# Layer 1 attention: short blocks of query rows share their buffers of exponentials, fp16 parts and transposed parts

## The chip, the core and the metric

The kernel runs on one core of one Trainium2 chip. The metric is the time of one execution in device microseconds. The numbers in the sections ahead of the result are from the kernel before the change: three timed runs and one profiled execution.

## What is computed

Two layers act on x, of shape (2, 1024, 512) in float32. Each one adds an attention branch and a feed-forward branch to its input, both fed with the layer norm of that input:

```python
xn = _layernorm(x, axis=-1)
x = x + _L0_attn_ref(xn, ...) + _L0_ffn_ref(xn, ...)
xn = _layernorm(x, axis=-1)
x = x + _L1_attn_ref(xn, Wq, Wk_down, Wv_down, Wk_up, Wv_up, Wo) + _L1_ffn_ref(xn, ...)
```

The change is in the attention of layer 1. It has 32 query heads of size 128, and 8 heads of keys and values which are built from a compressed form; four query heads share one head of keys. It is causal:

```python
scores = jnp.einsum('bhqd,bhkd->bhqk', q, k) * scale
scores = jnp.where(causal, scores, -1000000000.0)
attn = jax.nn.softmax(scores, axis=-1)
out = jnp.einsum('bhqk,bhkd->bhqd', attn, v)
return out.transpose(0, 2, 1, 3).reshape(b, s, H * D) @ Wo.T
```

## The kernel before

**Arithmetic.** float32 values are held as two fp16 parts, a high and a low one, and each product takes three matmul passes (`mm3`, recorded at L88): high by high, high by low, low by high.

**Units of work in layer 1.** The outer loop runs over 16 groups: 2 batches of 8 key heads. A group has 32 steps (`s`), and each step takes one *row block*: 32 query positions of the four heads, which makes 128 rows. Row block `s` sees `32 * (s + 1)` keys, so W goes from 32 to 1024 within a group. Four row blocks make one column `c` (`c = s // 4`, 0 to 7) of 128 query positions.

**One row block**, in the order in which it passes the engines:

- TensorE: scores into a PSUM bank `s` (four banks; L88 with `s<-K,Q`).
- VectorE: scale, mask and running minimum into the float32 buffer `P` (L268; above 512 keys also L272), with the minimum in `nm`.
- ScalarE: exponential in place, with the row sum (L276).
- VectorE: reciprocal (L289). ScalarE: times a constant (L290), then the high part into `Phl` (L295).
- GpSimd: a memset of the part of `Phl` that lies past W, up to the next multiple of 128 (L285; three of four row blocks need one).
- VectorE: the low part into `Phl` (L301), which reads `P` and `Phl`.
- SyncE's queue: a DMA that transposes `Phl` into `PT` (L303).
- TensorE: probabilities times values, per pair of row blocks (`group_av`, L328, into the one PSUM bank `av`). ScalarE and VectorE write that out as two parts `ao` (`evac`, L103 and L104), and TensorE multiplies `ao` by Wo (`wo_block`, L88 with `pp<-wo,ao`); VectorE adds the result to `acc` (L707).

**Buffers.** `T(tag, shape, bufs=n)` takes one of n buffers of that tag, and each is as large as the largest tile of the tag. `P` has 3, `Phl` has 3, `PT` has 3. One row block takes a whole `P` and a whole `Phl`, whatever its W. A pair of row blocks takes one `PT`. A buffer is free again when every instruction that used it is done: `P` after the low part (L301), `Phl` after the transposing DMA has landed, `PT` after `group_av`. So row block `s` needs the `P` and the `Phl` of row block `s - 3`, and pair j needs the `PT` of pair j - 3.

**Order.** The program names the work step by step: row block `s` in step `s`; the low part of the block before it in the same step; `group_av` of a pair three or four steps later (`AVD = 5`); `wo_block` three steps after that (`WOD = 10`). The projections of queries (`qproj`), of the next group's keys and values (`kv`) and the loads and splits of weights on GpSimd (`load_w`, `split_pool`, L94 to L96, L662) are hung on steps too. In the eight groups of batch 0 there is more of it: the Sinkhorn chain of layer 0's second batch on GpSimd and VectorE (`sk`, L522 to L564), its mixing on ScalarE and GpSimd (L613, L614), gating, the low-rank feed-forward block (`ffn_block`, L907, L912). When the program is built, a scheduler orders the instructions of each engine by a timeline of its own, in which a step waits where a buffer isn't free. On the chip each engine then runs its instructions in that fixed order and waits for semaphores.

## Time and profile before

| | |
|---|---|
| three timed runs | 1926.15, 1918.57, 1919.13 us; median 1919.13 |
| profiled execution | 1926.57 us, its span 1924.8 us |
| TensorE busy | 1743.7 us, 91% of the span, 11458 matmuls |
| VectorE busy | 1487.2 us, 77% |
| ScalarE busy | 1204.1 us, 63% |
| GpSimd busy | 902.4 us, 47% |
| first scores of layer 1 | at 268 us; the groups of batch 1 begin at 1147 us |

Read it so. All times in the traces count from the start of the span. A line of waits gives the engine that waited, its instruction, what ended the wait, the microseconds in total, how often, and the longest. A line of the timeline gives the start, the length, the engine, the line, the operation with its tiles, and in square brackets how long the engine was idle before it and what ended that. A line of a table of stretches gives the length and, for each engine, busy time with the number of instructions, then the granted TensorE clock (1.00 is full), the DMA engines' busy share and GB/s. Ends of matmuls are modelled.

### The profile page before, as it was taken

What the parts mean: (1) busy time and instruction counts of PE and PEld (TensorE: products, weight loads), DVE (VectorE), ACT (ScalarE), POOL (GpSimd) and SP (SyncE); (2) the same over time, 40 slices, a digit from 0 to 9 for tenths busy, and PEclk for the clock granted to TensorE, in tenths of its full rate; (3) what the DMA queues carried; (4) which work ended last, traced back from release to release, by engine and by line L of the source; (5) the groups of instructions that cost most, each with busy time, mean ns of one, the idle gap of its engine ahead of it and who ended that gap; (6) DMA issues with size and microseconds to landing.
All of it is one profiled execution on the core that took longest, in us unless ns stands there. A gap on an engine that the chain in (4) does not pass through costs nothing. (4 is left out here: it accounts for less than half of the span.)

```text
span 1924.8 us, 35319 instructions
## 1 busy us (share of the span) xinstructions
PE 1743.7 (91%) x11458; PEld 1050.0 (55%) x11458; DVE 1487.2 (77%) x4050; ACT 1204.1 (63%) x2917; POOL 902.4 (47%) x1540
## 2 busy tenths in 40 slices
PE   4766399999999989999899899999999999999998
PEld 3433146556556555555554456666566666656565
DVE  8888967987887868686965767777778787878675
ACT  4747755656566777866444556666666666666564
POOL 5657676676756554634612715151515152426100
PEclk9877799999999999999989999999999999999999
DMA  7425225566553746475744855665656565557455
GB/s 203 88 45 132 56 65 110 137 126 124 108 128 87 157 92 139 109 137 123 151 96 77 173 110 126 132 116 132 126 125 129 127 135 118 131 121 147 106 120 118
DMA packets 707308, 230.27 MB, mean 120 GB/s; under 512 B 689953, under 2 KB 690081, under 8 KB 707122
## 3 DMA queue, kind: packets, MB, share of 16 engines
q1 hardware_dynamic: 691666, 180.75, 46.3%
q0 software_dynamic: 13152, 43.07, 8.7%
q10 hardware_dynamic: 2304, 4.20, 0.7%
q8 instruction: 90, 1.47, 0.3%
q14 instruction: 96, 0.79, 0.2%
HBM read 52.81 MB, written 4.19 MB: 30 GB/s over the span
## 5 line engine op out<-in xcount | busy, mean ns | idle before, releaser
L301 DVE SCALAR_TENSOR_TENSOR Phl<-P,r,Phl 128x1024 f16<-128x1024 f32 (+31 forms) x515 | 469.8, 917 | 180.1 <-ACT Phl L295 168.4
L276 ACT ACTIVATE P<-P,nm 128x1024 f32<-128x1024 f32 (+31 forms) x528 | 392.3, 743 | 319.1 <-DVE nm L268 302.2
L328 PE MATMUL av<-PT,V 128*128 128x256 f16 x3648 | 456.6, 277 | 21.5 <-DMA PT<-Phl 13.0
L88 PE MATMUL s<-K,Q 128*128 128x512 f16 (+22 forms) x2400 | 446.8, 317 | 31.0 <-DVE P L272 19.5
L295 ACT ACTIVATE Phl<-P,r 128x1024 f16<-128x1024 f32 (+31 forms) x515 | 374.1, 733 | 109.1 <-DMA PT<-Phl 92.1
L328 PEld LDWEIGHTS <-V 128*128 128x128 f16 x3648 | 359.4, 99 | 121.8 <-DMA PT<-Phl 16.1
L88 PE MATMUL pp<-wo,ao 128*128 128x512 f16 x1536 | 373.6, 380 | 20.3 <-ACT ao L103 20.1
L285 POOL MEMSET Phl<- 128x192 f16 (+2 forms) x384 | 77.6, 205 | 657.1 <-DMA PT<-Phl 515.9
L88 PE MATMUL pp<-xT,wq 128*128 128x512 f16 x1536 | 375.1, 383 | 0.0
L88 PEld LDWEIGHTS <-Q 128*128 128x128 f16 x2400 | 222.9, 98 | 185.5 <-issue 44.6
L88 PEld LDWEIGHTS <-ao 128*128 128x128 f16 x1536 | 148.0, 98 | 175.9 <-ACT ao L103 27.7
L88 PEld LDWEIGHTS <-wq 128*128 128x128 f16 x1536 | 150.5, 99 | 169.1 <-issue 8.2
L268 DVE CUSTOM_DVE_ANT_0 P<-s,mask,nm 128x272 f32<-128x272 f32 (+15 forms) x256 | 157.0, 615 | 7.3 <-DVE P L272 1.0
L272 DVE TENSOR_SCALAR_CACHE_REDUCE P<-s 128x512 f32<-128x512 f32 (+15 forms) x272 | 152.0, 561 | 7.6 <-PE s L88 4.2
L94 POOL TENSOR_SCALAR f2k<-f2k 128x512 f32<-128x512 f32 x164 | 115.3, 704 | 88.0 <-DMA f2k<-in_Wq 46.3
L289 DVE RECIPROCAL r<-r 128x1 f32<-128x1 f32 x528 | 80.5, 156 | 77.2 <-ACT P L276 71.5
L290 ACT ACTIVATE r<-r 128x1 f32<-128x1 f32 x528 | 95.8, 193 | 66.6 <-DVE r L289 65.1
L268 DVE CUSTOM_DVE_ANT_0 P<-s,mask 128x32 f32<-128x32 f32 (+15 forms) x256 | 106.3, 430 | 13.2 <-PE s L88 10.6
L88 PEld LDWEIGHTS <-xT 128*128 128x128 f16 x864 | 65.1, 104 | 80.1 <-DMA xT<-h2k 43.5
L88 PE MATMUL pp<-cmp,xT 128*128 128x128 f16 (+2 forms) x720 | 88.1, 277 | 20.5 <-DMA xT<-h2k 15.8
L104 DVE SCALAR_TENSOR_TENSOR Q<-pp,Q 128x512 f16<-128x512 f32 x128 | 87.1, 681 | 25.3 <-ACT Q L103 25.2
L103 ACT ACTIVATE ao<-av 128x512 f16<-128x512 f32 x128 | 74.7, 584 | 47.6 <-PE av L328 47.3
(262 smaller groups left out, 2137.6 us busy)
## 6 DMA issues: line engine op xcount, KB each, us to landing
f2k<-in_Wq POOLq DMA_DIRECT2D x64, 256.0 KB, 3.4
f2k<-in_WoT POOLq DMA_DIRECT2D x64, 256.0 KB, 3.6
PT<-Phl SPq DMA_TRANSPOSE x528, 3.4
acc<-in_x SPq DMA_DIRECT2D x16, 256.0 KB, 5.2
f2k<-in_Wup POOLq DMA_DIRECT2D x16, 256.0 KB, 3.5
out<-acc ACTq DMA_DIRECT2D x16, 256.0 KB, 3.1
xr<-in_x SPq DMA_DIRECT2D x12, 256.0 KB, 5.1
f2k<-in_Wlat POOLq DMA_DIRECT2D x8, 256.0 KB, 6.5
```

The lines of the kernel that those rows point to most:

```text
L88: nc.tensor.matmul(dst, lhs(l), rhs(r), start=(i == 0 and j == 0), stop=(i == n - 1 and j == 2))
L94: G.tensor_scalar(stage, stage, scale, 1.0, ALU.mult, ALU.mult)
L104: return V.scalar_tensor_tensor(hl_lo, src, scale, hl_hi, ALU.mult, ALU.subtract)
L268: last_row[0] = V.tensor_tensor_reduce(Pm[:, o:o + w], pt[:, :w], mask[:, 512 - w:], -scale, first, ALU.add, ALU.min, nm[:, k:k + 1])
L272: last_row[0] = V.tensor_scalar(Pm[:, o:o + w], pt[:, :w], -scale, first, ALU.mult, ALU.min, accum_out=nm[:, k:k + 1])
L276: A.activation(Pm[:, :W], Pm[:, :W], AF.Exp, bias=last, scale=-1.0, accum_out=r[:, 0:1])
L285: G.memset(hl[:, :, W:], 0.0)
L289: V.reciprocal(r[:, 1:2], r[:, 0:1])
L290: A.activation(r[:, 1:2], r[:, 1:2], AF.Copy, scale=PSCALE)
L295: A.activation(hl[:, 0, :W], Pm[:, :W], AF.Copy, scale=r[:, 1:2])
L301: V.scalar_tensor_tensor(hl[:, 1, :W], Pm[:, :W], r[:, 1:2], hl[:, 0, :W], ALU.mult, ALU.subtract)
L328: nc.tensor.matmul(p, Vh(j, l), PT(r * nj + j), start=(j == 0 and k == 0), stop=(j == nj - 1 and k == 2))
```

## The change

For a column with `c < 2` (up to 256 keys) the four row blocks share one `P`, one `Phl` and one `PT`, each block with a quarter of it. For `c` of 2 and 3 (up to 512 keys) two row blocks share one `P` and one `Phl`, and the four of the column share one `PT`. From `c = 4` on, all is as it was. The number of buffers and their sizes are the same: 1024 float32 for `P`, 2048 fp16 for `Phl`, 4096 fp16 for `PT`. The shared tile is asked for at its first row block, and freed when all of its row blocks are done.

```diff
+    def share(got, n, k, make):
+        if k % n == 0:
+            got[0] = make()
+        return got[0][:, k % n]
+
+    P_of, hl_of = [None], [None]
+
-    def rows_exp(pieces, causal, scale):
+    def rows_exp(pieces, causal, scale, n, k):
...
-        Pm = T("P", [P, S], bufs=PB)
+        Pm = share(P_of, n, k, lambda: T("P", [P, n, S // n], bufs=PB))
...
-    def rows_pad(W):
-        n = -(-W // P)
-        hl = T("Phl", [P, 2 * S], F16, bufs=LB)[:, :2 * n * P].rearrange("p (l k) -> p l k", l=2)
-        if W < n * P:
+    def rows_pad(W, n, k):
+        m = -(-W // P)
+        hl = share(hl_of, n, k, lambda: T("Phl", [P, n, 2 * S // n], F16, bufs=LB))
+        hl = hl[:, :2 * m * P].rearrange("p (l k) -> p l k", l=2)
+        if W < m * P:
             G.memset(hl[:, :, W:], 0.0)
...
                     c, r = divmod(s, NR)
-                    if r % 2 == 0:
+                    n = 4 if c < 2 else 2 if c < 4 else 1
+                    if c < 4 and r == 0:
+                        PT = T("PT", [P, 2 * (c + 1), NR, P], F16, bufs=3)
+                        for k in range(2):
+                            PTs[g, 2 * c + k] = PT[:, :, 2 * k:2 * k + 2]
+                    elif c >= 4 and r % 2 == 0:
                         PTs[g, s // 2] = T("PT", [P, 2 * (c + 1), 2, P], F16, bufs=3)
...
-                             kvs[g]["K"], QR * (s + 1), True, SC1, PTs[g, s // 2][:, :, r % 2], False)
+                             kvs[g]["K"], QR * (s + 1), True, SC1, PTs[g, s // 2][:, :, r % 2], False, n, r)
```

`row_step` passes `n` and `k` on; layer 0 calls it with `n = 1`.

More of the change, by code (lines that the diff above doesn't have):

```diff
@@ L305, in tile_model, with row_step @@
     pending = []
-    def row_step(q=None, K=None, W=None, causal=None, scale=None, dst=None, pool=None):
+    def row_step(q=None, K=None, W=None, causal=None, scale=None, dst=None, pool=None, n=1, k=0):
         if q is not None:
@@ L315, in row_step @@
         if q is not None:
-            pending.append((*rows_exp(pieces, causal, scale), pool, rows_pad(W), dst))
+            pending.append((*rows_exp(pieces, causal, scale, n, k), pool, rows_pad(W, n, k), dst))
         if old:
```

## The prediction, made blind

> **What bounds the kernel now.** I read the busy times by stage first, then TensorE's waits, then the waits of the engines that feed it, then the timeline around TensorE's longest waits. By stage, in the table of stretches (TensorE's busy time is the second number, the granted clock the one after POOL's):

> ```profile
> 0.00:268.00 268.00, 163.23 (x998) 90.97 (x999) 221.37 (x679) 157.54 (x360) 177.15 (x204) 0.83 0.43 101
> 268.00:1147.00 879.00, 817.46 (x5397) 489.74 (x5397) 684.62 (x1841) 553.50 (x1381) 473.91 (x872) 0.97 0.57 120
> 1147.00:1925.00 778.00, 763.05 (x5064) 469.32 (x5062) 581.20 (x1531) 493.06 (x1177) 251.37 (x465) 1.00 0.60 125
> ```

> The first 268 us are layer 0, which the change doesn't touch; on TensorE the two builds have the same order until the first group's rows. In batch 1 TensorE is idle for 778.00 - 763.05 = 15 us. In batch 0 it is idle for 61.5 us at a clock of 0.97. So TensorE bounds layer 1, and no change of waits can win more than those 76 us and the missing clock. What ends TensorE's waits in batch 0:

> ```profile
> PE pp L88 <- ACT ao L103: 14.8, 12, 4.8
> PE s L88 <- DVE P L272: 11.4, 11, 2.9
> PE s L88 <- DVE nm L268: 9.1, 11, 2.0
> PE av L328 <- DVE ao L104: 8.0, 3, 4.3
> ```

> ScalarE and VectorE are late with single instructions, though neither is full. Who holds them up? In the waits of the whole execution, two lines name the transposing DMA, that is, a `Phl` buffer which isn't free:

> ```profile
> POOL Phl L285 <- DMA PT<-Phl: 515.9, 160, 12.5
> ...
> ACT Phl L295 <- DMA PT<-Phl: 92.1, 64, 6.1
> ```

> GpSimd's 516 us look large but gate little, since its work is mostly due much later. The 92 us on ScalarE matter more: its queue is in order, and `ao` stands behind the waiting high part. The longest such wait for a short row block, in the timeline:

> ```profile
> 685.05 0.45 ACT L295 ACTIVATE Phl<-P,r 128x192 f16<-128x192 f32 x1
> 685.41 0.19 ACT L290 ACTIVATE r<-r 128x1 f32<-128x1 f32 x1
> ...
> 688.65 0.48 ACT L295 ACTIVATE Phl<-P,r 128x224 f16<-128x224 f32 x1 [3.05 <-DMA PT<-Phl]
> ...
> 689.04 0.58 ACT L103 ACTIVATE ao<-av 128x512 f16<-128x512 f32 x1
> ...
> 689.67 1.04 PE L88 MATMUL pp<-wo,ao 128*128 128x512 f16 x2 [4.80 <-ACT ao L103]
> ```

> The high part of the 224-key block waits 3.05 us for the transpose of the 128-key block three before it; `ao` waits behind it, and TensorE 4.80 us behind that. Then the clock is lower for some microseconds:

> ```profile
> 690.00:694.00 4.00, 4.00 (x11) 1.45 (x10) 3.47 (x14) 2.98 (x10) 0.00 (x0) 0.50 0.01 2
> 694.00:698.00 4.00, 4.00 (x19) 1.81 (x18) 1.20 (x3) 2.23 (x7) 1.98 (x3) 0.82 0.00 0
> ```

> **The change part by part.**

> *Instructions.* Both builds have the same ones on every engine (22916 on TensorE, 3762 on VectorE, 2405 on ScalarE, 1543 on GpSimd, 622 on SyncE), of the same shapes. Only the instructions that do nothing but wait are fewer: VectorE 1147 to 922, ScalarE 689 to 584, GpSimd 505 to 446, TensorE 155 to 162. One that needn't wait takes 21 ns (the shortest at L301), so VectorE saves 225 x 0.021 = 4.7 us of sequencer time. It has 77% load and lies beside TensorE: taken as nothing, at most 5.

> *Buffers of exponentials (P).* VectorE frees them itself at L301, in its own order; no wait of the trace names them. Nothing directly, only through the order (below).

> *Buffers of parts (Phl), the main term.* Before, block s needs the transpose of block s-3. After, the four blocks of column 0 need the one of block 29 of the group before, column 1 that of block 30, blocks 8 and 9 that of block 31, 10 and 11 that of column 0, and so on: never a later one than before, and for columns 0 to 3 nearly always one that has long landed. Added up by row block, 73 of ScalarE's 92 us are for columns 0 to 3, half in each batch. What TensorE gets of it: I followed each of its waits back along what released it. It passes straight through such a `Phl` wait at 384.6 (0.85 us of TensorE idle), 402.5 (0.21), 689.7 (4.80, of which the `Phl` wait explains 3.05), 888.2 (1.43), 1039.6 (2.46), 1256.0 (0.77), 1350.9 (1.94), at 1443, 1536, 1629 and 1722 (0.27, 0.31, 0.31, 0.34) and at 1817 (0.60). Sum 12.5 us. With the first stall cut to 1.75 us the low clock behind it goes as well, since the stalls of 1.43 and 1.94 us were followed by a clock of 1.00: 4 x 0.50 + 4 x 0.18 = 2.7 us. Together 15.2. What is late next is VectorE's `nm` and TensorE's own `av`, so I take a fifth off: **-12 us**, between 0 (all of it comes late elsewhere) and -27 (the waits that have such a wait further back, another 12, go too).

> *Buffers of transposed parts (PT).* The same from another side: SyncE's queue waits for `av` now and then, and TensorE waits for `PT` 7.0 us in layer 1 (4.3 and 2.7). It falls free earlier for columns 0 to 3; for blocks 16 on, each pair needs the same or an older one. Nothing to -7; I take 0, since half of these waits are of long blocks. TensorE's reads of a half of the shared tile wait for their own two transposes only, so no new wait comes in.

> *Order.* With the buffers free, the scheduler sets short blocks earlier. TensorE's work between the scores of a pair and its `av`, counted in columns of 0.417 ns (score matmuls of 288 and 480 columns take 286 and 366 ns), grows for columns 2 and 3 in batch 1 (before 10 to 17 us; after, 15 to 22 in every second group and 13 to 19 in the others), while for the long blocks it moves by a microsecond either way, in some groups of batch 0 by -2 to -4. A loss: at a group's end VectorE now runs up to four minima of the next group (about 0.3 us each in the trace) and the write-out of `Q` (0.68) ahead of the last low part, and ScalarE one `Q` (0.58) and one exponential (0.4). That makes the last transpose about 1.9 us later. Its landing had 3 to 5 us to spare on average (least 0.1 in batch 0, 0.5 in batch 1). Price 0 to 1.5 us a group, 16 groups, 0 to +24; I take 0, since TensorE's distance for these blocks rises by about a microsecond too.

> *GpSimd.* Its memsets no longer wait, so weight splits, mixing and the chain follow each other without pause. That can hurt VectorE. The trace has such a stretch, GpSimd without a pause and VectorE in one low part of 320 keys, which alone takes 0.54 us (the shortest of its shape):

> ```profile
> 492.34 4.58 DVE L301 SCALAR_TENSOR_TENSOR Phl<-P,r,Phl 128x320 f16<-128x320 f32 x1
> 496.85 0.68 DVE L104 SCALAR_TENSOR_TENSOR ao<-av,ao 128x512 f16<-128x512 f32 x1
> ```
> ```profile
> 492.85 1.16 POOL L96 TENSOR_TENSOR wo<-f2k,wo 128x512 f16<-128x512 f32 x1
> 493.97 0.25 POOL L530 TENSOR_TENSOR sk<-sk 128x32 f32<-128x32 f32 x1
> 494.18 1.14 POOL L96 TENSOR_TENSOR wo<-f2k,wo 128x512 f16<-128x512 f32 x1
> ```

> Five low parts of batch 0 and one of batch 1 are stretched by over 2 us. TensorE then idled 3.5 us of 494 to 498 and had a clock of 0.64 until 502 (1.4 us): about 5 us. GpSimd's total work is the same, so I take as many such meetings as before: 0, with -5 x 5 and +5 x 10 as ends that I don't expect together. [...]

> *Sum.* Profiled execution 1926.6 - 12 = 1914.6 us. It lies 7.4 us above the median 1919.13, at the level of the slowest of the three runs; the same 12 us taken from the median give **1907 us**.

> **The rivals.** (About 0.5%, 9.6 us, is what a measurement of this kernel can tell from no change.)

> *A, my forecast*: ScalarE's waits for `Phl` go, TensorE's stalls behind them close. For: each of the twelve was followed to such a wait. 1907, from 1893 (-26) to 1909.

> *B, hidden anyway*: ScalarE, freed from the DMA, waits for VectorE's minima instead (already its largest wait, 302 us at L276), and TensorE stalls at the same points. For: in batch 1 it is 98% busy, and 9 of the 12 stalls are under 1.5 us. Then only the pieces before VectorE gain, a third: 1915, from 1910 to 1926.

> *C, slower: GpSimd without pauses holds VectorE's low parts.* Each further meeting as at 492 costs 5 us. Against 12 us of gain it decides from five new ones on (+13); one more in each of batch 0's groups gives 8 x 5 - 12 = +28, 1947; likeliest five to six, 1934. For: the memset waits were pauses at just the steps where `wo` is split. Against: the total is the same, and batch 1 had one such meeting.

> *D, slower: the last long block of a group comes late*, the order's price above: 16 x 1.5 - 12 = +12, 1931. Against: its distance on TensorE rose.

> That the change doesn't do what it says can be excluded: the build shows the waits gone.

> **How the numbers follow.** A 0.49, B 0.26, C 0.16, D 0.09. Faster by over 0.5% is A with a little of B: 0.50. Within 0.5% the rest of B and the weak ends of C and D: 0.27. Slower 0.23. The range for 8 in 10 leaves out the upper half of C and the lowest end of A: 1892 to 1932. A's own range is 1893 to 1909.

> **What would show it.** Right: ScalarE's `Phl` wait at L295 falls from 92 to about 20 us, GpSimd's at L285 from 516 to about 250; the stall of 4.8 us before `wo,ao` in the fifth group shrinks below 2, and `pp <- ACT ao` falls in both batches. For B: those waits fall and TensorE's idle time stays at 76 us. For C: more low parts over 2 us at L301. For D: more waits of `av` for `PT` at the ends of groups. I would be wrong if TensorE's idle time in layer 1 rose.

## The result, and the profile after

The changed kernel takes 1889.05 us (median of four runs, 1885.4 to 1894.29) against 1918.99 for the kernel before beside it (four runs): a ratio of 0.9841, 95% interval 0.9814 to 0.9867. That is 30 us less where 12 were forecast, and below the lower end of the range, 1892. Its profiled execution took 1894.29 us, the slowest of the four; the span is 1892.6 us. The program's lines are shifted: L268 became L276, L272 L280, L285 L294, L295 L304, L301 L310, L303 L312, L328 L337, and L88, L103 and L104 stay.

The table of stretches of the changed kernel, cut at its own first scores (267.2 us) and its own start of batch 1 (1122.4 us):

```profile
0.00:267.20 267.20, 162.47 (x1000) 91.15 (x1001) 220.23 (x680) 157.33 (x361) 177.27 (x209) 0.83 0.43 101
267.20:1122.40 855.20, 803.85 (x5397) 486.28 (x5397) 673.86 (x1840) 545.49 (x1380) 481.06 (x872) 0.99 0.59 124
1122.40:1892.60 770.20, 761.36 (x5067) 470.05 (x5064) 582.45 (x1531) 488.06 (x1177) 249.30 (x460) 1.00 0.59 127
```

Batch 0 is 23.8 us shorter and batch 1 7.8 us; the untouched head gives 0.8. TensorE's idle time in layer 1 falls from 76.5 to 51.4 + 8.8 = 60.2 us. Its busy time in batch 0 falls too, from 817.5 to 803.9 us with the same matmuls, while the granted clock rises from 0.97 to 0.99: in this pair of profiles, 13.6 of batch 0's 23.8 us are clock.

What ended TensorE's waits in batch 0, and the two waits for `Phl` over the whole execution (engine, instruction, releaser; microseconds, times, longest):

```profile
PE s L88 <- DVE P L280: 13.6, 12, 2.3
PE s L88 <- DVE nm L276: 9.3, 12, 2.0
PE pp L88 <- ACT ao L103: 6.6, 7, 1.9
PE av L337 <- DMA PT<-Phl: 5.7, 5, 2.3
```
```profile
POOL Phl L294 <- DMA PT<-Phl: 427.6, 128, 18.8
...
ACT Phl L304 <- DMA PT<-Phl: 6.6, 7, 1.9
```

The wait for `ao` led the list before, with 14.8 us; it has 6.6 now, and none of its waits is longer than 1.9. ScalarE's wait for `Phl` is nearly gone, 92.1 to 6.6 us. The waits for VectorE's `P` and `nm` are about as long as before.

The fifth group at the place of the 4.80 us stall, in the timeline of the changed kernel:

```profile
676.61 0.86 ACT L304 ACTIVATE Phl<-P,r 128x224 f16<-128x224 f32 x2
677.38 0.57 ACT L103 ACTIVATE ao<-av 128x512 f16<-128x512 f32 x1
677.85 0.52 ACT L304 ACTIVATE Phl<-P,r 128x288 f16<-128x288 f32 x1
...
678.27 0.59 PE L88 MATMUL pp<-wo,ao 128*128 128x512 f16 x2
```

The high part of the 224-key block carries no square bracket: it waits for nothing. `ao` follows it at once, and so does TensorE.

**A split that the experiments use.** Every run lists its span and its granted clock. Span times clock is counted as the time at full speed, and the rest as lost to the clock. This is bookkeeping: where TensorE idles at a low clock, the loss is counted although nothing is lost. Over the 65 runs of the kernel before that the experiments were timed against (mean span 1919.0 us) that is 1858.4 + 60.5 us; over eight of the changed kernel (1887.6 us) 1836.2 + 51.4. Some 44 us of the loss lie in the head of both. So the change is 22 us of waits and 9 us of clock. The means of four to ten runs have standard errors of about 1 to 3.5 us in either part, so differences of a few microseconds between two kernels are not clear of noise.

### The profile page after: what moved, and what is told of

The parts are those of the page before. It is cut to its first block, busy times and chain, and to the rows that moved or that the text cites. A ratio compares the mean times of both kernels' runs of the same rounds, so it can differ in the third digit from the quotient of the medians.

```text
span 1892.6 us, 34936 instructions
## 1 busy us (share of the span) xinstructions
PE 1727.7 (91%) x11458; PEld 1047.5 (55%) x11458; DVE 1476.5 (78%) x4050; ACT 1190.9 (63%) x2917; POOL 907.6 (48%) x1540
## 5 line engine op out<-in xcount | busy, mean ns | idle before, releaser
L310 DVE SCALAR_TENSOR_TENSOR Phl<-P,r,Phl 128x1024 f16<-128x1024 f32 (+31 forms) x515 | 461.6, 908 | 91.6 <-ACT Phl L304 84.3
L88 PE MATMUL s<-K,Q 128*128 128x512 f16 (+22 forms) x2400 | 443.7, 317 | 35.8 <-DVE P L280 22.7
L337 PE MATMUL av<-PT,V 128*128 128x256 f16 x3648 | 451.0, 275 | 15.7 <-DMA PT<-Phl 11.7
L337 PEld LDWEIGHTS <-V 128*128 128x128 f16 x3648 | 357.7, 99 | 108.1 <-DMA PT<-Phl 9.7
L304 ACT ACTIVATE Phl<-P,r 128x1024 f16<-128x1024 f32 (+31 forms) x515 | 369.6, 731 | 22.1 <-DMA PT<-Phl 6.6
L88 PE MATMUL pp<-wo,ao 128*128 128x512 f16 x1536 | 372.9, 380 | 9.5 <-ACT ao L103 8.5
L88 PE MATMUL pp<-xT,wq 128*128 128x512 f16 x1536 | 370.3, 380 | 2.2 <-DVE K L104 1.1
L294 POOL MEMSET Phl<- 128x192 f16 (+2 forms) x384 | 72.4, 205 | 582.9 <-DMA PT<-Phl 427.6
L88 PEld LDWEIGHTS <-Q 128*128 128x128 f16 x2400 | 222.9, 98 | 194.0 <-issue 46.9
L88 PEld LDWEIGHTS <-wq 128*128 128x128 f16 x1536 | 149.8, 98 | 168.0 <-issue 5.6
L88 PEld LDWEIGHTS <-ao 128*128 128x128 f16 x1536 | 148.6, 98 | 162.5 <-ACT ao L103 12.4
L276 DVE CUSTOM_DVE_ANT_0 P<-s,mask,nm 128x272 f32<-128x272 f32 (+15 forms) x256 | 157.4, 616 | 11.7 <-PE s L88 5.2
L280 DVE TENSOR_SCALAR_CACHE_REDUCE P<-s 128x512 f32<-128x512 f32 (+15 forms) x272 | 152.6, 561 | 9.5 <-PE s L88 5.8
L299 ACT ACTIVATE r<-r 128x1 f32<-128x1 f32 x528 | 96.1, 192 | 63.5 <-DVE r L298 62.8
L103 ACT ACTIVATE ao<-av 128x512 f16<-128x512 f32 x128 | 74.9, 585 | 80.1 <-PE av L337 76.8
L104 DVE SCALAR_TENSOR_TENSOR Q<-pp,Q 128x512 f16<-128x512 f32 x128 | 87.1, 681 | 42.4 <-ACT Q L103 42.3
L276 DVE CUSTOM_DVE_ANT_0 P<-s,mask 128x32 f32<-128x32 f32 (+15 forms) x256 | 105.0, 429 | 14.2 <-PE s L88 13.5
L103 ACT ACTIVATE Q<-pp 128x512 f16<-128x512 f32 x128 | 74.3, 581 | 59.6 <-PE pp L88 59.6
L716 DVE SCALAR_TENSOR_TENSOR acc<-pp,acc 128x512 f32<-128x512 f32 x128 | 86.8, 679 | 27.3 <-PE pp L88 26.6
```

The lines of the kernel that those rows point to most:

```text
L88: nc.tensor.matmul(dst, lhs(l), rhs(r), start=(i == 0 and j == 0), stop=(i == n - 1 and j == 2))
L103: A.activation(hl_hi, src, AF.Copy, scale=scale)
L104: return V.scalar_tensor_tensor(hl_lo, src, scale, hl_hi, ALU.mult, ALU.subtract)
L276: last_row[0] = V.tensor_tensor_reduce(Pm[:, o:o + w], pt[:, :w], mask[:, 512 - w:], -scale, first, ALU.add, ALU.min, nm[:, k:k + 1])
L280: last_row[0] = V.tensor_scalar(Pm[:, o:o + w], pt[:, :w], -scale, first, ALU.mult, ALU.min, accum_out=nm[:, k:k + 1])
L299: A.activation(r[:, 1:2], r[:, 1:2], AF.Copy, scale=PSCALE)
```

## Experiments

Theory 1: the gain is the missing wait for `Phl`. Rivals: another of the three buffers carries it; the scheduler's new order carries it; the clock's part is luck.

### One buffer at a time, and all but the parts

`row_step` gets two counts instead of one, `n` for the exponentials `P` and `m` for the parts `Phl`, and the transposed parts `PT` are shared or not by their own condition:

```diff
-                    n = 4 if c < 2 else 2 if c < 4 else 1
-                    if c < 4 and r == 0:
+                    n, m = 1, 4 if c < 2 else 2 if c < 4 else 1   # parts alone
+                    if False and r == 0:                          # PT per pair, as before
```

Parts alone:

> Only the buffers of parts (Phl) are shared (four row blocks up to 256 keys, two up to 512); exponentials and transposed parts as before. Theory 1 (the gain is ScalarE's missing waits for Phl): nearly the whole change, 1889 to 1896 us; ScalarE's wait for the transposing DMA falls from 92 to under 15 us and TensorE loses about 85 us in batch 0 instead of 108. Rival 2 (the transposed parts set the order of the transposes, Phl alone moves the wait to SyncE's queue): 1905 to 1919 us. Rival 3 (any new order of the scheduler would have done it): no tie to the Phl wait, anywhere from 1885 to 1925 us.

Exponentials alone:

> Only the buffers of exponentials (P) are shared. Theory 1: no gain, 1914 to 1924 us, with ScalarE's Phl wait still near 92 us. Rival 3 (new order): a clear move away from 1919 us, by 8 us or more.

Transposed parts alone:

> Only the tiles of transposed parts (PT) are shared by a column's four blocks. Theory 1: at most the 7 us of TensorE's waits for PT, 1912 to 1922 us. Rival 2 (transposed parts carry the gain): 1889 to 1905 us.

Exponentials and transposed parts, without the parts:

> Exponentials and transposed parts are shared, the parts (Phl) are not: the whole change but for its main term. Theory 1: 1912 to 1922 us, ScalarE's Phl wait still 80 to 95 us, the low clock in batch 0 still about 40 us long. Rival 2 or 3: 1905 us or less.

| shared | median us | ratio to before, 95% | at full speed | lost to the clock |
|---|---|---|---|---|
| parts | 1902.51 | 0.9905 (0.9871 to 0.9938) | 1840.7 | 59.9 |
| exponentials | 1922.18 | 1.0004 (0.9982 to 1.0026) | 1858.2 | 61.6 |
| transposed parts | 1926.54 | 1.0047 (1.0022 to 1.0072) | 1865.5 | 60.1 |
| exponentials, transposed parts | 1952.93 | 1.0177 (1.0134 to 1.0220) | 1877.2 | 74.2 |

The parts are the main term, but no theory has this table: they alone give 17 us of 30, and the other two together cost 33. Nor does the length of ScalarE's wait for `Phl` order the times. It is 5.2 us with the parts alone, 126.0 with the exponentials alone, which are as fast as before, and 59.0 with the transposed parts alone, which are slower. The profile says what the 33 are. With exponentials and transposed parts shared, ScalarE and TensorE wait longer than in the kernel before (92.1 and 20.1 us over the whole execution):

```profile
ACT Phl L304 <- DMA PT<-Phl: 111.1, 73, 5.4
...
PE pp L88 <- ACT ao L103: 37.9, 21, 5.2
```

and in the timeline, in the eleventh group (the first line is VectorE's, the last TensorE's):

```profile
1367.62 1.64 DVE L310 SCALAR_TENSOR_TENSOR Phl<-P,r,Phl 128x416 f16<-128x416 f32 x1 [0.65 <-ACT Phl L304]
...
1377.44 0.72 ACT L304 ACTIVATE Phl<-P,r 128x512 f16<-128x512 f32 x1 [5.44 <-DMA PT<-Phl]
1378.06 0.58 ACT L103 ACTIVATE ao<-av 128x512 f16<-128x512 f32 x1
...
1378.70 1.03 PE L88 MATMUL pp<-wo,ao 128*128 128x512 f16 x2 [5.22 <-ACT ao L103]
```

It is the old kind of stall, longer. The scheduler, free of the other two buffers, has set the 512-key block's high part ahead of `ao`; its `Phl` is the one of the 416-key block three before, whose low part ended at 1369.26. The transpose had landed only 8 us later. In groups 10 to 15, TensorE's waits before `wo,ao` that last over 1 us add up to between 1.3 and 6.3 us each. Each kernel so far has an order of its own, so buffers and order had to be separated.

### The other two pairs, and both kernels again

> Exponentials and parts shared, transposed parts as before. The parts alone gave 1902.5 us, so 13 us of the change are still to be placed; over its runs the span splits into 1840.7 us at full speed (span times granted clock) and 59.9 us lost to the clock, against 1836.3 and 51.4 with the whole change. Theory P (free exponentials let the minima of short blocks run ahead, which only pays once the parts are free): 1886 to 1893 us, loss to the clock near 51. Theory T (the transposed parts do it): 1898 to 1906 us. Theory C (the clock's part is luck of where its windows fall): 1892 to 1900 us here and without the exponentials alike.

> Parts and transposed parts shared, exponentials as before. Theory P: 1898 to 1906 us. Theory T: 1886 to 1893 us, loss to the clock near 51. Theory C: 1892 to 1900 us.

Parts and exponentials: 1899.62 us, ratio 0.9885 (0.9859 to 0.9910), 1840.7 + 55.5 us. Parts and transposed parts: 1902.56, 0.9906 (0.9887 to 0.9926), 1840.1 + 60.3 us. Neither P nor T holds. C is nearest, though the second time lies above its range: at full speed both equal the parts alone, neither reaches the whole change, and what differs between them is the clock.

> The changed kernel once more, for a second profile and more runs. If the halved clock is set by the kernel's own stalls, its four periods in layer 1 (at 367, 797, 965 and 1054 us) come again within a few us and the loss to the clock stays at 50 to 53 us. If it is luck (theory C), they move and the loss spreads by 5 us and more between the runs.

> The kernel before once more, for a second profile. If the stalls set the clock: the ten periods of low clock in layer 1 (at 368, 498, 573, 637, 689, 958, 975, 1040, 1064, 1078 us) come again, 22 us lost in them. If it is luck: at least a third of them are missing or elsewhere, and the loss differs by over 5 us.

The changed kernel gave 1889.66 us (0.9844, 0.9822 to 0.9867) and again 51.4 us of clock on average, but from 47.2 to 56.7 in its four runs (the clock is listed to 0.001, which is 1.9 us). Three of its four low periods came again, 2, 5 and 8 us earlier in an execution that was itself up to 7 us ahead; one was missing, and two were new. Of the ten of before, nine came again within 6 us, one was missing and one was new; 18.8 us were lost in them instead of 22.2. So the two signs part. The places say that the stalls set the low clock; the spread of over 9 us between runs is the one that was named for luck. Both are at work. The profile that the prediction was made from was an unlucky one: it lost 69 us of its span to the clock (1 - 0.964 of 1924.8 us), against 60.5 on average.

### Which columns

All three buffers shared, for columns 0 and 1 only, or for 2 and 3 only (`n = 4 if c < 2 else 1`; `n = 2 if 2 <= c < 4 else 1`).

> All three buffers shared, but only for columns 0 and 1 (up to 256 keys). ScalarE's waits for Phl before lie to two thirds at these columns (35 us against 18 at columns 2 and 3). If the gain follows the waits: two thirds of it, 1896 to 1903 us. If it needs the whole chain of rings free: 1903 to 1915 us.

> All three shared, but only for columns 2 and 3 (257 to 512 keys). If the gain follows the waits: one third, 1906 to 1913 us. If it needs the whole chain: 1913 to 1922 us.

Columns 0 and 1: 1909.77 us, 0.9927 (0.9901 to 0.9954), 1842.7 + 63.5. Columns 2 and 3: 1908.10, 0.9931 (0.9908 to 0.9955), 1847.8 + 59.1. In time the halves are alike, which speaks against a gain in proportion to the waits. At full speed they are 15.7 and 10.6 us, nearer to the two thirds and one third; the first half loses 3 us of clock, the second gains 1. Read again from the trace, ScalarE's waits are 60 us at columns 0 and 1 and 20 at columns 2 and 3, not 35 and 18. Each of the two kernels has an order of its own too, so these runs do not tell the columns' waits from the order.

### One buffer of parts more

```diff
-FB, HB, PB, LB, XB, WB = 4, 3, 3, 3, 4, 5
+FB, HB, PB, LB, XB, WB = 4, 3, 2, 4, 4, 5
```

> The kernel before with four buffers of parts instead of three and two of exponentials instead of three, nothing shared, the same memory. If ScalarE's wait for Phl is the cause and any slack in that ring is enough: its wait falls from 92 to under 45 us and the time to 1900 to 1910 us. If two buffers of exponentials hold the minima back, or one buffer more is too few: 1915 us or more.

1952.90 us, 1.0178 (1.0126 to 1.0231). ScalarE's wait falls to 12.2 us, as expected, and the time rises all the same: layer 0, which uses `P` too, is 14 us longer, and TensorE's waits for `PT` rise from 13.0 to 37.3 us. Two things were changed at once, and the loss of a buffer of exponentials seems to cost more than a fourth of parts can give, so this says nothing of the parts.

### The old order with the new buffers

This takes the order away from the question. The instructions of both kernels are the same, one for one; the program ties each to its predecessor in a given order of its engine, here the one of the kernel before:

```diff
+            tc.add_manual_dep(ins, last.name, mybir.DependencyInfo(
+                mybir.DependencyClass.NoSync, mybir.DependencyReason.DATA), reason="pin_order")
```

> The buffers of the changed kernel, but every engine runs its instructions in exactly the order of the kernel before: only waits are missing, nothing is moved. Theory W (missing waits carry the gain): the stalls of TensorE that have a wait for Phl in their chain, 21 us in the profile of before, go, and some 4 us of halved clock with them: 1892 to 1902 us. Theory O (the scheduler's new order carries it): 1910 to 1919 us.

1893.49 us, 0.9844 (0.9805 to 0.9882): the whole gain, 1838.3 + 52.0 us, with every engine's instructions in the old order. In the trace all 11458 matmuls, and the instructions of the other engines, follow each other as in the kernel before. What is missing is the wait for `Phl`:

```profile
ACT Phl L304 <- DMA PT<-Phl: 5.4, 5, 2.2
```

Theory O falls. The reverse, the new order on the old buffers, was not tried.

The same order with fewer buffers shared:

> The order of the kernel before on every engine, with only the buffers of parts shared. Theory W1 (the waits for Phl carry the whole gain; the 13 us that the parts-only kernel lacked are its own order): 1887 to 1897 us. Theory W2 (waits for the other two buffers carry the rest): 1898 to 1907 us.

> The order of the kernel before, with exponentials and transposed parts shared and the parts as before. Theory W1: 1914 to 1922 us, so that the 33 us which the same buffers cost in their own order are that order's. Theory W2: 1903 to 1912 us.

> All buffers of the changed kernel, in the order that the scheduler made for the kernel with only the parts shared. If the 13 us are that order's: 1897 to 1906 us, as with the parts alone. If they are waits for exponentials and transposed parts: 1885 to 1893 us.

> The order of the kernel before, with parts and transposed parts shared, exponentials as before. If SyncE's waits for transposed parts are the rest of the gain: 1888 to 1895 us, as with all three. If the shared exponentials are: 1896 to 1900 us, as with the parts alone.

| order | shared | median us | ratio to before, 95% | at full speed | lost to the clock |
|---|---|---|---|---|---|
| before's | all three | 1893.49 | 0.9844 (0.9805 to 0.9882) | 1838.3 | 52.0 |
| before's | parts | 1897.71 | 0.9889 (0.9869 to 0.9908) | 1842.9 | 52.6 |
| before's | parts, transposed parts | 1893.74 | 0.9865 (0.9842 to 0.9889) | 1840.6 | 53.0 |
| before's | exponentials, transposed parts | 1916.77 | 0.9986 (0.9963 to 1.0010) | 1855.1 | 60.3 |
| parts-only kernel's | all three | 1899.70 | 0.9911 (0.9882 to 0.9939) | 1840.2 | 58.9 |

In the old order the parts give 21 us, not 17 (the intervals overlap), and the time lies between the ranges of W1 and W2. Without the parts the gain is gone, since 0.9986 is not clear of no change, and ScalarE waits again:

```profile
ACT Phl L304 <- DMA PT<-Phl: 74.9, 57, 4.2
```

So the other two cost nothing in the old order, and the 33 were the price of an order. The parts-only kernel's order takes some 1900 us even with all three buffers free, and loses 59 us to the clock: what it lacked, or most of it, was its order's too.

What do the transposed parts add in the old order? The waits of SyncE's queue for `group_av` to free a `PT`, first in the kernel before:

```profile
SPq L303 <- PE av L328: 29.8, 17, 7.8
```

and in the old order with the parts alone shared:

```profile
SPq L312 <- PE av L337: 39.6, 29, 4.2
```

With the parts free, part of the wait moves on to SyncE, which waits for `PT` 10 us longer. In the old order with transposed parts shared the line falls below 1 us, with and without the exponentials. By the medians that is worth 4 us (1897.71 to 1893.74, and 1893.49 with the exponentials as well), at full speed 2.3 us; the intervals overlap, so this is a size and not a proof.

## Why the prediction was right or wrong

**Right: the place and the mechanism.** ScalarE's wait at the high part fell to 6.6 us (about 20 forecast), the stall of the fifth group went, and `pp <- ACT ao` fell in both batches, from 14.8 to 6.6 and from 5.3 to 2.0. The missing waits carry the gain, as the run in the old order shows. The *order* term, taken as 0 between 0 and +24, was 0: the old and the new order take 1893.49 and 1889.05 us with the same buffers, and their intervals lie on each other. That was luck in part. Two other orders that the scheduler made cost, by the medians, 6 us (1899.70 against 1893.49, all three shared) and 36 us (1952.93 against 1916.77, without the parts).

**Wrong: three sizes.** First, the main term, the waits behind `Phl`. The forecast had 12.5 us in twelve stalls, took a fifth off, which made 10, and left the stalls that have such a wait further back to the bound. The parts alone in the old order gain 1858.4 - 1842.9 = 15.5 us at full speed. TensorE's instructions are the same and in the same order there, so its stalls can be compared one by one. The twelve were 14.3 us (13.3 in the second profile of before). They shrink to 3.2 us with the parts alone, and to 2.3 with all three buffers, so nothing had to be taken off. And the list of twelve was short by at least one, a stall of 4.31 us which was there in both profiles of before. Its block has 576 keys:

```profile
1061.50 0.77 ACT L295 ACTIVATE Phl<-P,r 128x576 f16<-128x576 f32 x1 [2.94 <-DMA PT<-Phl]
...
1062.31 0.82 DVE L301 SCALAR_TENSOR_TENSOR Phl<-P,r,Phl 128x576 f16<-128x576 f32 x1 [2.95 <-ACT Phl L295]
...
1064.38 1.04 PE L328 MATMUL av<-PT,V 128*128 128x256 f16 x4 [4.31 <-DVE ao L104]
```

VectorE's `ao` stands behind the low part that waits for this high part. After the change, the block (number 17) takes the buffer that blocks 12 and 13 shared, where it took that of block 14. With the parts alone in the old order the stall is 1.5 us long, and the low period that began at 1064.1 us is gone. All other stalls together moved by less than 1 us, single ones by up to 2 us either way, as they do between two executions of the kernel before. (Columns 0 to 3 have 80 of ScalarE's 92 us by the trace, where the forecast read 73; its sum did not use that number.)

Second, the clock: 2.7 us before the fifth, counted behind one stall, where the runs give 60.5 - 51.4 = 9.1. The next lines are a table of stretches of the kernel before, cut along the low periods (length, then TensorE's busy time; the number after POOL's is the clock):

```profile
569.11:572.52 3.41, 1.24 (x7) 0.58 (x7) 2.35 (x7) 3.32 (x12) 2.90 (x6) 1.00 0.50 110
572.52:575.93 3.41, 3.41 (x9) 1.22 (x8) 2.97 (x11) 1.27 (x6) 3.22 (x8) 0.50 0.91 200
633.96:637.37 3.41, 1.55 (x8) 0.58 (x6) 3.29 (x5) 0.00 (x0) 2.41 (x3) 1.00 0.08 18
637.37:640.79 3.42, 2.82 (x12) 1.58 (x12) 3.35 (x11) 2.84 (x9) 1.78 (x3) 0.50 1.03 231
...
685.20:688.62 3.42, 0.00 (x0) 0.00 (x0) 0.42 (x1) 0.40 (x2) 0.00 (x0) 1.00 1.08 139
688.62:692.03 3.41, 2.36 (x6) 0.89 (x7) 2.65 (x10) 2.77 (x9) 0.93 (x3) 0.50 0.01 2
692.03:695.44 3.41, 3.41 (x9) 1.21 (x8) 1.66 (x6) 1.18 (x4) 0.00 (x0) 0.50 0.00 0
695.44:698.86 3.42, 3.42 (x19) 1.68 (x18) 1.54 (x3) 3.09 (x10) 2.81 (x4) 1.00 0.02 5
```

Each of the ten low periods follows a stretch of 3.41 us in which TensorE worked little (for 0 to 1.2 us of it, by the matmuls' starts and columns), and not only after the longest stall: in those from 569 and from 634 us it was still busy for 1.24 and 1.55 us (this column counts each matmul with its modelled end; by starts and columns it is 1.08 and 1.18 us). There were 13 stretches at half clock in layer 1 before, 13 x 1.71 = 22.2 us, and four after, 6.8 us; in the second profiles, 11 and five. I had looked at what lay behind the stalls that I had priced, found 1.00 behind some of them, and not asked what lay ahead of the other low periods. The trace of before would have told it (last section).

Third, the transposed parts, "nothing to -7; I take 0": 2 to 4 us, as above, not clear of noise.

Together 15.5 + 9 us, and 2 to 4 more if the third is real, of 30 to 31 measured. The end of the bounds, -27, was nearer than the value taken: for the fifth, for the stalls further back, for the clock and perhaps for `PT`, I had taken the cautious end, and the errors all pointed the same way.

**Missed beside it:** GpSimd's wait was to halve and fell to 427.6 us only. In the changed order its memsets seem to reach the long blocks earlier and wait there instead, up to 18.8 us at a time; in the old order the wait is 350.8. The two orders take the same time, so it gates little, as forecast.

**The rivals.** B (hidden anyway) needed TensorE's idle time to stay at 76 us; it is 60. D (the last long block late) needed more waits of `av` for `PT`: 12 of them, 13.0 us, before, and 8, 11.7 us, after. C needed more stretched low parts: with over 2 us there are two in batch 0 and one in batch 1, where there were five and one. The longest one after, in the timeline, has 448 keys; another of that shape, in the kernel without shared parts, takes 0.67 us:

```profile
689.74 4.78 DVE L310 SCALAR_TENSOR_TENSOR Phl<-P,r,Phl 128x448 f16<-128x448 f32 x1
690.15 1.28 POOL L623 TENSOR_TENSOR acc<-acc,f2k 128x512 f32<-128x512 f32 x1
...
691.38 1.16 POOL L96 TENSOR_TENSOR wo<-f2k,wo 128x512 f16<-128x512 f32 x1
...
692.69 1.26 POOL L623 TENSOR_TENSOR acc<-acc,f2k 128x512 f32<-128x512 f32 x1
```

The meetings still happen, and freeing GpSimd did not multiply them. Again the low part, 4.78 us long, lasts through several GpSimd instructions of 1.16 to 1.28 us. No run here isolates what stretches it.

## What to carry to other kernels

A short tile that takes a whole slot of a ring wastes the ring's depth. Where an engine that keeps its order writes that slot, the wait holds all that is queued behind it (here ScalarE's 3.05 us held `ao`, and TensorE idled 4.80 us before `wo,ao`), and each engine's stalls should be followed back past the first hop. Free the ring that is waited for: freeing its neighbours alone let the scheduler run further ahead into the tight ring, and that order cost 33 us. Price stalls of TensorE with the clock that they cost (here 9 us of 31), over every stretch in which it works little.

## What the runs showed of the hardware

In time, every cell of layer 1 that was followed by half clock had 2.1 us or more without work, in one gap or several: ahead of the low period at 975 us in the profile of before it is one gap of 2.21 us, ahead of that at 368 us there are gaps of 0.26, 0.87 and 1.60 us.

This could explain part of the spread of a kernel's own runs: the number of low cells would depend on where the grid cuts a stall. Slid over the profile of before in steps of 50 ns, the grid and a mark of 0.37 give 10 to 15 low cells in layer 1, 12.5 on average, or 21 us (11.0, or 19 us, in the second profile); over the two profiles of the changed kernel 2 to 11 and 3 to 9, on average 6.5 and 6.7, or 11 us. The difference is 8 to 10 us, an estimate; the runs gave 9. Its first half, the cells of the kernel before, could have stood in the prediction.
